# A spectral attention kernel: products of factors and modes in four 64x64 tiles, and sums over modes begun on VectorE

## The chip, the cores and the metric

The kernel runs on one core of a Trainium2 chip. The metric is device time in microseconds; the median of three runs of the kernel before is 557.22 us (555.65 to 564.92). Times inside a run come from one profiled execution, whose span, from the first to the last instruction, is 555.1 us.

## The reference, cut to what matters

Two layers of a Fourier neural operator with attention, over x of shape (2, 56, 128, 128): 2 batches, 56 planes of 128x128. Each layer first normalises groups of pixels and then computes, cut to what matters here:

```
def spectral_conv(x, w, b):                    # M1 = M2 = 16
    xf = jnp.fft.rfft2(x, norm='forward')
    top = jnp.einsum('bihw,iohw->bohw', xf[:, :, :M1, :M2], _c(w[0]))
    bot = jnp.einsum('bihw,iohw->bohw', xf[:, :, -M1:, :M2], _c(w[1]))
    ...
k, q, v = (fno_layer(xn, ...) for K, Q, V)     # back by irfft2, 1x1 skip added; 8 heads
scores = jnp.einsum('baks,bals->bakl', qh, kh) * scale
attn = jax.nn.softmax(scores, axis=-1)
out = jnp.einsum('bakl,bals->baks', attn, vh)
out = fno_layer(out, P)
att = inorm(out + xa, gan, ban)
h = fno_layer(inorm(att, g2, b2), M0, norm=True, act=True)
h = fno_layer(h, M1, norm=True)
y = inorm(h, gmo, bmo) + att                   # the layer adds x to it
```

Only 32x16 complex modes of each plane pass through the weights. So the kernel works on modes: 1024 real numbers per plane, held as 128 partitions by 8 groups of 56 planes.

## The kernel before, in words

For each batch `b` and layer `L` the work is a chain of stages, each written as a Python generator. `_woven` and `_with` mix the generators of two batches; the tile framework then orders the instructions of each engine and places the semaphores, so the order on an engine is not exactly that of the text.

*Modes* (`modes_chain`, L456). Statistics, normalisation, then the transform over the two axes (`to_modes`, L381). The modes of a batch end in `xf` (128 x 448 = 8 groups `t` of 56 planes, and 8 columns of zeros), copied by ScalarE at L498. The two halves of 64 partitions, `e` = 0 and 1, hold different modes.

*Gram* (`gram`, L506 to L514) multiplies every image row with itself, 128 matmuls at L511.

*Scores* (`scores`, L566). For each pair of groups, `t` and `t + 1`, 32 matmuls at L597 multiply 64x64 factors `WU` with the 64x56 modes, for 8 heads, two groups `k` and two halves `e`. The row half of the array is the half of the modes, the column half is the half of PSUM that is written. Before, both are `e`, so of the four 64x64 quadrants of the array only two are in use, in alternation:

```
e = k ^ r
T.matmul(
    p[64 * e : 64 * e + 64, k, K * a : K * a + K], lhsT=WUv[64 * e : 64 * e + 64, t + k, a, :],
    rhs=xv[64 * e : 64 * e + 64, t + k, :], start=True, stop=True,
    tile_position=(64 * e, 64 * e), skip_group_check=True,
)
```

ScalarE copies the 128x896 result out of PSUM (L602) into one of two buffers `UX`; `scored` (L583) multiplies the buffer of two steps earlier by the modes, at L578, and adds up all eight groups in one PSUM bank. A last product (also L578, with `gc`) closes the sum, and L637 on VectorE, the start of the softmax, waits for it. `p` comes from `pair()`, three PSUM buffers of two banks shared by nearly all stages; `bank()` has two of one bank.

*Values, softmax, mix, heads* follow (L611 to L697), with L620 using all four quadrants for 64x256 products, and L680 and L690 for the mixing.

*Norms* (`norms_chain`, L699). The variances of the outputs are sums over the modes, each mode counted twice but those that are their own mirror (`count`, 1 or 2 per partition and group). `sums` (L439) takes 8 matmuls of one column, one per group, with the 56 planes as the stationary side. It is called for `u` (L713) and for the squares `sqy` (L715); L717 on VectorE reads the two columns, L721 takes roots on ScalarE, L431 builds a diagonal, and L436 spreads it over the partitions. The norms of batch 0 run together with the scores of batch 1; the norms of batch 1 run together with `gelu` of batch 0.

*First and second layer of the perceptron* (`gelu`, L771: synthesis L751, mixing L766, GELU L819, statistics L821 on VectorE, turning back L801, transform L789; `h_chain`, L830). In `h_chain`, `sums` is called for s2 and s1 (L852 and L853), after L843 (modes), `multiply` (L419, copied at L424), the squares (L847) and L848; L855 reads the result.

*End* (`end`, L886). L916 on VectorE and L918 on GpSimd make the outputs; `moved` issues their loads and stores on SP's queue (L896). For layer 0 `turned` (L354) brings them into the next layer's form. `prepare` (L235), with L270 to L302, makes the factors of layer 1's weights on GpSimd while layer 0 runs.

SP's queue issues DMAs in order: the image loads, two rows of `gvr` per batch and layer (L554, one per half), then the loads and stores of L896. `P[b]` is one big buffer per batch; its columns are reused: the planes (0 to 7168), `SG` and `MI` of the scores (7168 to 7840), the outputs of the perceptron (all 8192).

Of the kernel before, what the change touches and what calls it, by code (L numbers as in the profile page):

```python
# [39 lines left out]
ALU = mybir.AluOpType  # L40
AX = mybir.AxisListType
# [7 lines left out]
_PARTS = {}  # L49
for _name, _n in (  # L50
    ("ident", N), ("fw", 32), ("fh", N), ("gw", N), ("group", N), ("dup", N), ("ext", N), ("fold", 64),
    ("raw", 56), ("count", 8), ("syn", 1), ("same", 32), ("m8", 8), ("m16", 16), ("n2", 1), ("fx", N), ("gh", 2 * N),
):
    _PARTS[_name] = (sum(n for _, n in _PARTS.values()), _n)
N_CONST = sum(n for _, n in _PARTS.values())
# [2 lines left out]
def _constants():  # L58
    pos = np.arange(N)
    th = 2 * np.pi * np.outer(pos, np.arange(16)) / N  # L60
    fw = np.concatenate([np.cos(th), -np.sin(th)], 1) / N

    def over_h(h):
        ph = 2 * np.pi * np.outer(h, _KY) / N
        cy, sy = np.cos(ph), np.sin(ph)
        return np.concatenate([cy, -sy, sy, cy], 1) / N, np.stack([np.r_[cy.T, -sy.T], np.r_[sy.T, cy.T]], 1)

    at = 4 * (pos % 32) + pos // 32
    fh = over_h(at)[0]
    g, s, e, c = at // 16, at // 8 % 2, at // 2 % 4, at % 2  # L70
    by_layer = []
    for hx, hz in (
        (16 * g + 8 * c + 4 * s + e, pos.reshape(4, 4, 2, 4).transpose(1, 0, 3, 2)),
        (16 * g + 4 * c + 8 * s + e, pos.reshape(4, 2, 4, 4).transpose(2, 0, 3, 1)),
    ):
        z = over_h(hz.reshape(-1))[1]
        by_layer += [over_h(hx)[0], np.concatenate([z, z], 0).reshape(N, 2 * N)]
    twice = np.where(np.arange(16) == 0, 1.0, 2.0)
    both = np.stack([np.cos(th) * twice, -np.sin(th) * twice]).reshape(2, N, 2, 8)
    gw = np.tile(both.transpose(2, 0, 3, 1).reshape(32, N), (4, 1))  # L80
    p = np.arange(N)
    group = (p[:, None] // 4 == p // 4) / 4.0
    k = np.arange(K)
    dup, ext, fold = np.zeros((N, N)), np.zeros((N, N)), np.zeros((N, 64))
    for r in range(2):
        dup[k, 64 * r + k] = 1
        ext[k, 64 * r + k] = 1
        ext[k, 64 * r + K] = -1
        fold[64 * r + k, k] = 1

    c, kx = p // 16 % 2, p % 16
    row = 8 * (p // 32)[:, None] + np.arange(8)
    edge = kx[:, None] == 0
    own = np.where(edge, 0.5, np.ones((N, 8)))
    mirror = np.where(edge & (row != 16), 0.5, np.zeros((N, 8)))
    count = np.where(edge & (row != 16), 1.0, np.full((N, 8), 2.0))
    dc = np.where(edge & (row == 0), 0.0, np.ones((N, 8)))
    re, im = (c == 0)[:, None] * 1.0, (c == 1)[:, None] * 1.0
    raw = np.stack(
        [own, mirror, -mirror, count * dc * N * re, count * dc * N * im, dc * re, dc * im], 1  # L100
    ).reshape(N, 56)

    ky2, e2 = p % 32, p // 64
    edge2 = (8 * e2[:, None] + np.arange(8)) == 0
    parts = {
        "ident": np.eye(N), "fw": fw, "fh": fh, "gw": gw, "group": group, "dup": dup, "ext": ext,
        "fold": fold, "raw": raw,
        "count": np.where(edge2 & (ky2 != 16)[:, None], 1.0, 2.0),
        "syn": np.where(edge2 & (ky2 == 16)[:, None], 2.0, 1.0)[:, :1],
        "same": (ky2[:, None] == np.arange(32)) * 1.0,  # L110
        "m8": (p[:, None] % 8 == np.arange(8)) * 1.0,
        "m16": (p[:, None] // 8 == np.arange(16)) * 1.0,
        "n2": np.full((N, 1), 1.0 / N**2),
    }
    whole = np.concatenate([parts[n] for n in _PARTS if n in parts] + by_layer, 1)
    return {"all": np.ascontiguousarray(whole, np.float32)}
# [50 lines left out]
def fno_layers(ctx: ExitStack, tc: tile.TileContext, x, out, weights, small, const):  # L167
# [19 lines left out]
    def little(name, shape):  # L187
        return sm.tile(shape, F32, name=name)

    def grid(flat, n=8):  # L190
        return flat.rearrange("p (t k) -> p t k", t=n)
# [244 lines left out]
        T.matmul(p[:, : n * K], lhsT=ones[:K, :], rhs=dg, start=True, stop=True)  # L436
        return p[:, : n * K].rearrange("p (n k) -> p n k", n=n)

    def sums(p, col, of, start, stop):  # L439
        for t in range(8):  # L440
            T.matmul(
                p[:K, col : col + 1], lhsT=of[:, K * t : K * t + K], rhs=C["count"][:, t : t + 1],
                start=start and t == 0, stop=stop and t == 7, skip_group_check=True,
            )

    def padded(name, of, row):
# [9 lines left out]
    def modes_chain(L, b, stats, st):  # L456
        mv, gs, gv, sh = (little(f"{n}{b}", [N, k]) for n, k in (("mv", 2), ("gs", 2), ("gv", 1), ("sh", 1)))
        V.bn_aggr(mv, stats.rearrange("p n s -> p (n s)"))
        V.scalar_tensor_tensor(mv[:, 1:2], mv[:, 0:1], mv[:, 0:1], mv[:, 1:2], ALU.mult, ALU.add)
        yield 1.5  # L460
        p = bank()
        T.matmul(p[:, :2], lhsT=C["group"], rhs=mv, start=True, stop=True)
        V.tensor_copy(gs, p[:, :2])
        V.tensor_tensor(gv, gs[:, 0:1], gs[:, 0:1], ALU.mult)
        V.tensor_tensor(gv, gs[:, 1:2], gv, ALU.subtract)
        S.activation(gv, gv, AF.Sqrt, bias=eps)
        V.reciprocal(gv, gv)
        V.scalar_tensor_tensor(sh, gs[:, 0:1], -1.0, gv, ALU.mult, ALU.mult)
        mid = half[b][:, :1792]
        midv = grid(mid, 32)  # L470
        turned_rows = plane[b].rearrange("p (h q) k -> p q h k", q=4)
        wide = P[b][:, 7168 : 7168 + N]
        for j in range(4):
            i = 14 * j
            v = plane[b][:, :, i : i + 14]
            if j % 2:
                S.activation(v, v, AF.Identity, bias=sh, scale=gv)
            else:
                V.tensor_scalar(v, v, gv, sh, ALU.mult, ALU.add)
            yield 3.0 if j == 0 else 0.8  # L480
            p = bank()
            for q in range(4):
                T.matmul(  # L483
                    p[32 * q : 32 * q + 32, :448].rearrange("p (h i) -> p h i", h=32), lhsT=C["fw"],
                    rhs=turned_rows[:, q, :, i : i + 14], start=True, stop=True, tile_position=(0, 32 * q),
                    skip_group_check=True,
                )
            V.transpose(
                midv[:, :, i : i + 14].rearrange("p m i -> p i m"), p[:, :448].rearrange("p (h i) -> p i h", h=32),
            )  # L490
        G.tensor_copy(wide, gv.to_broadcast([N, N]))
        for c in range(2):
            G.tensor_scalar(wide[:, 64 * c + K : 64 * c + K + 1], sh, -1.0, None, ALU.mult)
        yield 2.2
        xf = sp.tile([N, 456], F32, name=f"xf{b}")
        G.memset(xf[:, 448:], 0.0)
        p = to_modes(mid, C["fx"])
        S.copy(xf[:, :448], p)  # L498

        p = bank()  # L500
        T.matmul(p[:, :N], lhsT=wide, rhs=ident, start=True, stop=True)
        gvr = little(f"gvr{b}", [N, N])
        S.copy(gvr, p[:, :N])
        st.update(xf=xf, gvr=gvr)

    def gram(b, st):  # L506

# [58 lines left out]
    def scores(L, b, st):  # L566
# [16 lines left out]
        def scored(t):  # L583
            u = R["UX"][t // 2 % 2]
            for k in range(2):
                score(
                    xf[:, K * (t + k) : K * (t + k) + 64], grid(u[:, 448 * k : 448 * k + 448]), start=(t + k == 0),
                    stop=False,
                )

        for t in range(0, 8, 2):
            p = pair()
            for r in range(2):
                for a in range(HEADS):
                    for k in range(2):
                        e = k ^ r
                        T.matmul(  # L597
                            p[64 * e : 64 * e + 64, k, K * a : K * a + K], lhsT=WUv[64 * e : 64 * e + 64, t + k, a, :],
                            rhs=xv[64 * e : 64 * e + 64, t + k, :], start=True, stop=True,
                            tile_position=(64 * e, 64 * e), skip_group_check=True,  # L600
                        )
            S.copy(R["UX"][t // 2 % 2].rearrange("p (k m) -> p k m", k=2), p[:, :, :448])  # L602
            yield 2.0
# [95 lines left out]
    def norms_chain(L, b, st):  # L699
# [10 lines left out]
        yield 0.8  # L710
        p = bank()
        T.matmul(p[:K, 0:1], lhsT=st["gb"], rhs=C["n2"][:K], start=True, stop=False, skip_group_check=True)
        sums(p, 0, u, False, False)  # L713
        yield 0.4
        sums(p, 1, sqy, False, True)  # L715
        k3, tm = (little(f"{n}{b}", [K, k]) for n, k in (("k3", 3), ("tm", 1)))
        V.tensor_scalar(k3[:, 0:1], p[:K, 0:1], EPS, None, ALU.add)  # L717
        V.tensor_scalar(k3[:, 1:2], p[:K, 0:1], d["gan2"][:K], EPS * EPS, ALU.mult, ALU.add)
# [111 lines left out]
    def h_chain(L, b, st):  # L830
# [18 lines left out]
        yield 1.6  # L849
        p = bank()  # L850
        T.matmul(p[:64, 2:4], lhsT=C["fold"], rhs=mv, start=True, stop=True, skip_group_check=True)
        sums(p, 1, s2, False, False)  # L852
        sums(p, 0, s1, False, True)  # L853
        c4, f1, r3 = little(f"c4{b}", [K, 4]), little(f"f1{b}", [K, 4]), little(f"r3{b}", [K, 2])
        V.tensor_copy(c4, p[:K, :4])  # L855
        g_, f_, u_, w_ = (f1[:, k : k + 1] for k in range(4))
# [168 lines left out]
```

## Time and profile before

| what | value |
|---|---|
| median of three runs | 557.22 us (555.65, 557.22, 564.92) |
| span of the profiled execution | 555.1 us |
| TensorE busy (matmul, weight load) | 457.0 us (82%), 316.3 us (57%) |
| VectorE, ScalarE, GpSimd busy | 337.0, 190.2, 184.3 us |
| mean granted clock of TensorE | 0.901 |
| L597, matmul records and busy time | 1024, 35.9 us |
| L441, matmul records and busy time | 256 (two rows of 128), 7.9 + 7.2 us |
| L578, matmul records and busy time | 144 (128 + 16), 17.5 + 2.4 us |
| HBM traffic | 24.69 MB read, 14.68 MB written |

A row of instruction groups reads: line, engine, operation, output <- inputs, shape and count, then busy time in us and mean ns of one, then how long the engine was idle before them and who ended it. A matmul in fp32 shows as two records, each with a weight load (PEld) and a matmul (PE). The chain of waits is the work that ended last, followed back from the end; its lines are the start in us, the length in us and the work.

### The profile page before, as it was taken

The page shows a single profiled execution, that of the slowest core. Times are in us where ns is not written, and L with a number is a line of the kernel's source. Part 1 is how long each engine was busy: PE and PEld are TensorE (multiplying, and loading weights), DVE is VectorE, ACT ScalarE, POOL GpSimd, SP SyncE. Part 2 cuts the span into 40 slices and gives each one's busy share as a digit, 9 for nine tenths or more (in the row PEclk, how much of TensorE's full clock was granted, in tenths as well). Part 3 has the DMA queues.
Part 4 walks back from the last instruction along what each step waited for, and adds up shares of the span by engine and source line. Part 5 has one row for each costly group of instructions (what it writes and reads, how often), then busy time and mean ns, then how long its engine had stood idle before and what let it go on. Part 6 is the DMA issues. An engine that isn't in the chain of part 4 may idle for free.

```text
span 555.1 us, 14768 instructions
## 1 busy us (share of the span) xinstructions
PE 457.0 (82%) x6630; PEld 316.3 (57%) x6630; DVE 337.0 (61%) x577; ACT 190.2 (34%) x238; POOL 184.3 (33%) x194
## 2 busy tenths in 40 slices
PE   2447889799999999798688859989999999979390
PEld 1423858669685555455563447768967556535250
DVE  0576478932717665869459995841253865677751
ACT  2344132063437556233103314124454656602000
POOL 2460424920271000065456871630000000035566
PEclk9999689899998999988667959989999999988586
DMA  8993000050000000056144541030000000017687
GB/s 202 213 197 58 4 2 2 5 145 4 2 3 1 1 2 1 1 166 198 53 132 133 168 127 14 2 105 4 2 2 2 1 1 2 2 33 225 191 230 285
DMA packets 16303, 40.58 MB, mean 73 GB/s; under 512 B 2528, under 2 KB 3296, under 8 KB 16224
## 3 DMA queue, kind: packets, MB, share of 16 engines
q1 hardware_dynamic: 15520, 38.25, 25.5%
q10 hardware_dynamic: 720, 1.39, 1.0%
q8 instruction: 52, 0.85, 0.6%
q14 instruction: 11, 0.09, 0.1%
HBM read 24.69 MB, written 14.68 MB: 71 GB/s over the span
## 4 chain that ended last, share of the span: by engine, by line
PE 43%; DVE 26%; DMA 8%; ACT 7%; POOL 7%; issue 5%; SPq 2%; POOLq 0%; ACTq 0%; DVEq 0%
PE pair L766 5%; DVE X L550 4%; PE pair L801 4%; PE pair L751 4%; PE pair L597 4%; DVE stats L373 4%; PE bank L511 3%; PE bank L578 3%; DMA C<-const_all 3%; DMA X<-store 3%; POOL P L918 3%; PE bank L690 3%; PE bank L789 2%; PE bank L483 2%; DMA xr<-store 2%
## 5 line engine op out<-in xcount | busy, mean ns | idle before, releaser
L821 DVE BATCH_NORM_STATS2 stats<-P 128x6 f32<-128x512 f32 x64 | 40.5, 681 | 19.3 <-ACT P L819 19.2
L916 DVE SCALAR_TENSOR_TENSOR P<-P,hs,pair 128x1024 f32<-128x1024 f32 x32 | 40.0, 1269 | 18.7 <-PE pair L766 18.7
L918 POOL TENSOR_TENSOR X<-P,xr 128x1024 f32<-128x1024 f32 x16 | 39.9, 2500 | 30.5 <-DVE P L916 16.5
L550 DVE TENSOR_TENSOR X<-X,gvr 120x1024 f32<-120x1024 f32 x32 | 49.3, 1568 | 0.0
L373 DVE BATCH_NORM_STATS2 stats<-P 128x6 f32<-128x448 f32 x64 | 35.7, 610 | 20.1 <-ACT P L368 10.1
L819 ACT ACTIVATE P<-pair 128x1024 f32<-128x1024 f32 x32 | 32.6, 1026 | 32.0 <-PE pair L766 31.3
L395 POOL MEMSET WT<- 128x256 f32 x4 | 1.3, 313 | 121.0 <-PE bank L789 88.3
L766 PE MATMUL pair<-X,Be 57*64 57x512 f32 x256 | 41.1, 742 | 0.0
L511 PEld LDWEIGHTS bank<-P 128*64 128x64 f32 (+1 forms) x1024 | 37.1, 158 | 2.9 <-issue 2.6
L511 PE MATMUL bank<-P 128*64 128x56 f32 (+1 forms) x1024 | 38.7, 244 | 0.0
L801 PEld LDWEIGHTS pair<-C,P 120*128 120x128 f32 x256 | 26.8, 143 | 20.9 <-issue 12.3
L766 PE MATMUL pair<-X,Bs 57*64 57x512 f32 x256 | 37.5, 627 | 0.0
L751 PE MATMUL pair<-C,WT 32*128 32x128 f32 x512 | 26.7, 319 | 11.3 <-DVE P L916 5.5
L597 PE MATMUL pair<-xf,WU 64*64 64x56 f32 x1024 | 35.9, 220 | 0.0
L597 PEld LDWEIGHTS pair<-xf,WU 64*64 64x64 f32 x1024 | 32.8, 134 | 5.0 <-issue 3.9
L751 PEld LDWEIGHTS pair<-C,WT 32*128 32x128 f32 x512 | 21.6, 214 | 23.6 <-issue 9.1
L801 PE MATMUL pair<-C,P 120*128 120x120 f32 x256 | 34.3, 277 | 0.4 <-ACT P L819 0.2
L341 POOL TENSOR_TENSOR WT<-tc,C 128x1024 f32<-128x1024 f32 x8 | 26.5, 3341 | 20.0 <-ACT tc L335 11.9
L802 ACT COPY WT<-pair 128x896 f32<-128x896 f32 x32 | 28.8, 906 | 12.5 <-PE pair L801 12.3
L363 PE MATMUL pair<-C,X 56*128 56x56 f32 x256 | 17.5, 292 | 18.6 <-DMA X<-x 12.8
L371 ACT COPY P<-pair 128x896 f32<-128x896 f32 x16 | 14.4, 902 | 46.7 <-PE pair L365 46.7
L365 PE MATMUL pair<-C,X 120*128 120x120 f32 x128 | 20.3, 313 | 10.2 <-POOL X L918 9.2
(249 smaller groups left out, 868.8 us busy)
## 6 DMA issues: line engine op xcount, KB each, us to landing
X<-x SPq DMA_DIRECT2D x16, 448.0 KB
xr<-x SPq DMA_DIRECT2D x32, 224.0 KB
store<-X SPq DMA_DIRECT2D x32, 224.0 KB
out<-P SPq DMA_DIRECT2D x32, 224.0 KB
xr<-store SPq DMA_DIRECT2D x16, 224.0 KB
X<-store SPq DMA_DIRECT2D x16, 224.0 KB
C<-const_all ACTq DMA_DIRECT2D x1, 621.0 KB
stage<-weights ACTq DMA_DIRECT2D x1, 544.0 KB
```

The costliest lines, as they stand in the source:

```text
L373: V.bn_stats(stats[:, 2 * g + s, :], dst[:, 448 * s : 448 * s + 448])
L511: T.matmul(p[u : u + m, :K], lhsT=P[b][:, K * i : K * i + m], rhs=plane[b][:, i, :], start=(i < 2), stop=(i == N - 1), tile_position=(0, u ...
L550: V.tensor_tensor(v, v, _bc(st["gvr"][:120], 1, 8), ALU.mult)
L597: T.matmul(p[64 * e : 64 * e + 64, k, K * a : K * a + K], lhsT=WUv[64 * e : 64 * e + 64, t + k, a, :], rhs=xv[64 * e : 64 * e + 64, t + k, ...
L751: T.matmul(both[j // 2][:, j % 2, N * e : N * e + N], lhsT=Z[32 * j : 32 * j + 32, o : o + N], rhs=C["gw"][32 * j : 32 * j + 32, :], start ...
L766: T.matmul(p[64 * c : 64 * c + 64, r, :], lhsT=Bs[q, :], rhs=X2[q, b, s : s + 4, :].rearrange("p e w -> p (e w)"), start=False, stop=True, ...
L801: T.transpose(p[:, r, N * e : N * e + 120], h3[:120, o : o + N], ident[:120, :120])
L802: S.copy(hT[v].rearrange("p r e c k -> p (r e) c k"), p.rearrange("p r (e c k) -> p (r e) c k", e=4, c=2)[:, :, :, :K],)
L819: S.activation(h3, both[v].rearrange("p r m -> p (r m)"), AF.Gelu)
L821: V.bn_stats(stats[:, 4 * A + 2 * v + r, :], h3[:, 512 * r : 512 * r + 512])
L916: V.scalar_tensor_tensor(h3, h3, st["hs"], both[v].rearrange("p r m -> p (r m)"), ALU.mult, ALU.add)
L918: G.tensor_tensor(dst, h3, back(n), ALU.add)
```

## The change

Three things.

1. *Four quadrants.* At L597 the loop runs over heads, then `k`, then `e`, and the PSUM half is `o = e ^ k`: an even group is written to the half it came from, an odd one to the other. Four matmuls in a row use the four quadrants.
2. *A copy of the modes with swapped halves.* As the odd groups of the product lie in the other half, L578 needs the modes of odd groups there too: `xs`, columns 7840 to 8072 of `P[b]`, is filled by two DMAs on SP's queue right after `xf`, and its last 8 columns are zeroed on GpSimd.
3. *Sums.* `sums` adds the eight groups on VectorE first, into a 128x56 tile, and then takes two matmuls of one column: the added groups with 2.0, and the first group with -1.0 where a mode is its own mirror. The constant `count` shrinks from 8 columns to 2.

The diff, cut to its core:

```
-        "count": np.where(edge2 & (ky2 != 16)[:, None], 1.0, 2.0),
+        "count": np.concatenate([np.full((N, 1), 2.0), -1.0 * (edge2 & (ky2 != 16)[:, None])[:, :1]], 1),
...
-    def sums(p, col, of, start, stop):
-        for t in range(8):
+    def sums(p, col, of, start, stop, name):
+        r = little(name, [N, K])
+        V.tensor_reduce(r, of.rearrange("p (t k) -> p k t", t=8), AX.X, ALU.add)
+        for j, part in enumerate((of[:, :K], r)):
             T.matmul(
-                p[:K, col : col + 1], lhsT=of[:, K * t : K * t + K], rhs=C["count"][:, t : t + 1],
-                start=start and t == 0, stop=stop and t == 7, skip_group_check=True,
+                p[:K, col : col + 1], lhsT=part, rhs=C["count"][:, 1 - j : 2 - j], start=start and j == 0,
+                stop=stop and j == 1, skip_group_check=True,
             )
...
         S.copy(xf[:, :448], p)
+        xs = P[b][:, 7840:8072]
+        G.memset(xs[:, 224:], 0.0)
+        for e in range(2):
+            q, o = slice(64 * e, 64 * e + 64), slice(64 - 64 * e, 128 - 64 * e)
+            nc.sync.dma_start(
+                out=xs[o, :224].rearrange("p (u k) -> p u k", k=K),
+                in_=xf[q, :448].rearrange("p (u v k) -> p u v k", v=2, k=K)[:, :, 1, :],
+            )
...
                 score(
-                    xf[:, K * (t + k) : K * (t + k) + 64], grid(u[:, 448 * k : 448 * k + 448]), start=(t + k == 0),
-                    stop=False,
+                    (xf[:, K * t : K * t + 64], st["xs"][:, K * t // 2 : K * t // 2 + 64])[k], grid(u[:, 448 * k : 448 * k + 448]),
+                    start=(t + k == 0), stop=False,
                 )
...
-            for r in range(2):
-                for a in range(HEADS):
-                    for k in range(2):
-                        e = k ^ r
+            for a in range(HEADS):
+                for k in range(2):
+                    for e in range(2):
+                        o = e ^ k
                         T.matmul(
-                            p[64 * e : 64 * e + 64, k, K * a : K * a + K], lhsT=WUv[64 * e : 64 * e + 64, t + k, a, :],
+                            p[64 * o : 64 * o + 64, k, K * a : K * a + K], lhsT=WUv[64 * e : 64 * e + 64, t + k, a, :],
                             rhs=xv[64 * e : 64 * e + 64, t + k, :], start=True, stop=True,
-                            tile_position=(64 * e, 64 * e), skip_group_check=True,
+                            tile_position=(64 * e, 64 * o), skip_group_check=True,
                         )
```

The four calls of `sums` (L713, L715, L852, L853) get a tile name as well. In the order that the framework gives the built kernel, the memset of L395 for batch 1 in layer 0 stands ahead of L270 and L271 on GpSimd, and the second sum of batch 1 at L715 has its reduce behind four statistics of L821 on VectorE. Lines after the edits move by 2 to 10; L597 becomes L607, L578 L588, L441 L443 and the reduce is L441.

More of the change, by code (lines that the diff above doesn't have):

```diff
@@ L51 @@
     ("ident", N), ("fw", 32), ("fh", N), ("gw", N), ("group", N), ("dup", N), ("ext", N), ("fold", 64),
-    ("raw", 56), ("count", 8), ("syn", 1), ("same", 32), ("m8", 8), ("m16", 16), ("n2", 1), ("fx", N), ("gh", 2 * N),
+    ("raw", 56), ("count", 2), ("syn", 1), ("same", 32), ("m8", 8), ("m16", 16), ("n2", 1), ("fx", N), ("gh", 2 * N),
 ):
@@ L503, in modes_chain @@
         S.copy(gvr, p[:, :N])
-        st.update(xf=xf, gvr=gvr)
+        st.update(xf=xf, xs=xs, gvr=gvr)
     def gram(b, st):
@@ L712, in norms_chain @@
         T.matmul(p[:K, 0:1], lhsT=st["gb"], rhs=C["n2"][:K], start=True, stop=False, skip_group_check=True)
-        sums(p, 0, u, False, False)
+        sums(p, 0, u, False, False, f"ru{b}")
         yield 0.4
-        sums(p, 1, sqy, False, True)
+        sums(p, 1, sqy, False, True, f"rq{b}")
         k3, tm = (little(f"{n}{b}", [K, k]) for n, k in (("k3", 3), ("tm", 1)))
@@ L851, in h_chain @@
         T.matmul(p[:64, 2:4], lhsT=C["fold"], rhs=mv, start=True, stop=True, skip_group_check=True)
-        sums(p, 1, s2, False, False)
-        sums(p, 0, s1, False, True)
+        sums(p, 1, s2, False, False, f"ru{b}")
+        sums(p, 0, s1, False, True, f"rq{b}")
         c4, f1, r3 = little(f"c4{b}", [K, 4]), little(f"f1{b}", [K, 4]), little(f"r3{b}", [K, 2])
```

## Prediction

> **What bounds the kernel now.** I read the page first: its chain of waits is 43% TensorE and 26% VectorE, so neither engine is the bound everywhere and each stage has to be looked at alone. The two rows of the product that the change rearranges:
>
> ```profile
> L597 PE MATMUL pair<-xf,WU 64*64 64x56 f32 x1024 | 35.9, 220 | 0.0
> L597 PEld LDWEIGHTS pair<-xf,WU 64*64 64x64 f32 x1024 | 32.8, 134 | 5.0 <-issue 3.9
> ```
>
> 1024 records stand for 512 matmuls: an fp32 matmul shows as two records (the program issues 4 steps x 32 matmuls x 2 batches x 2 layers). They keep TensorE busy for 36 us, but the page's chain gives L597 only 4%, some 20 us. Only those 20 us can be saved directly. So next, the chain in order of time, at the scores of batch 1, layer 0:
>
> ```profile
> 132.19 1.14 PE pair L419 x32
> 133.33 1.87 PE pair L597 x64
> 135.19 0.86 PE bank L441 x15
> 136.06 0.86 PE bank L578 x8
> 136.92 0.78 PE bank L441 x16
> 137.70 2.00 PE pair L597 x64
> 139.71 0.91 PE bank L578 x8
> 140.61 2.00 PE pair L597 x64
> 142.62 0.48 PE bank L436 x2
> 143.10 2.00 PE bank L578 x18
> ```
>
> For 13 us TensorE alone carries the path, and the softmax (L637, 145.33) waits for its last matmul. The same ten rows stand at 392.24 to 403.15 for layer 1. Both things that the change touches, L597 and the sums (L441), lie here. The sums of the second perceptron layer are on the path too:
>
> ```profile
> 207.03 1.10 PE pair L751 x32
> ...
> 208.66 1.02 PE pair L766 x8
> 209.67 0.21 PE bank L851 x2
> 209.88 1.67 PE bank L441 x32
> ```
>
> **What sets the pace of L597.** From chain rows: L441 loads 56 columns into one tile and takes 1.67/32 = 52 ns a record, 0.93 ns a column. L597 takes 1.87/64 = 29.2 ns a record with two tiles side by side, so 58 ns for each tile, 0.91 ns per column of its 64-column load: weight loads set its pace. Do four quadrants load and stream side by side? L766 is such a case: 1.02/8 = 128 ns a record of 512 columns, 0.25 ns a column; L578 with two tiles of 224 columns takes 0.86/8 = 108 ns, 0.48 ns. Four tiles are nearly twice as fast as two. L751 (four row tiles, loads of 128 columns) takes 1.10/32 = 34 ns, so loads overlap as well. And where the last L597 of one burst meets L620, which uses all four quadrants, the timeline has both in the same 60 ns:
>
> ```profile
> 109.88 0.43 PE L620 MATMUL pair<-WT,xf 64*64 64x256 f32 x2
> 109.93 0.23 PE L597 MATMUL pair<-xf,WU 64*64 64x56 f32 x2
> ```
>
> What no row shows is a long run faster than 29 ns a record.
>
> **What the Trainium skill says.** "TensorEngine Tiling (Array Packing)", Key Properties: tiles work independently, and different ones load and multiply at once; the rows above agree. "TensorE: Matmul & The Clock Gate", The mechanism: weight loads overlap running matmuls only if their row groups differ. The trace differs: L511 (128x64, both tiles on all rows) does 36 records in 1.19 us, 33 ns, like L597. Same page, "Wait — 56ns, not 53.3ns?": matmul starts don't come closer than about 25 ns; no stretch here tells. "SBUF — State Buffer", Who interferes with whom: tensor_reduce never contends with GpSimd, but two-input VectorE instructions do; the latter is seen (L861, one column, took 2.18 us under L918).
>
> **The change, part by part.**
>
> *Quadrants.* If a round of four takes the 58 ns of a round of two, 64 records take 0.93 us, not 1.87 to 2.00. Bounds: 0.93 (full overlap), 1.60 (25 ns a record, an estimate from the page), 1.87 (none). I take 0.95.
>
> *Sums.* 16 calls; each loses 16 records (0.83 us) and keeps 4 (0.21), and gains one reduce of 448 elements with a stride of 56. Nearest row: L639, a contiguous reduce of 224 in 377 ns; L702, 448 elements in 624. So 0.65 at pace 1, and about 1.1 if the stride costs double, which no row shows; I take 0.8.
>
> *Copy of the modes.* Two DMAs per batch and layer on SP's queue, and two little memsets on POOL. Nearest row: L554, also SBUF to SBUF, issue 0.56 us each; landing I put at 2 to 4 us (the page "DMA: Bandwidth & Descriptors", Anatomy of one DMA, has a fixed 2.0). Cover, layer 0: the modes are copied at 54.3 and 84.4, and L578 first needs them at 111.4 and 136. Layer 1: SP reaches the first pair after the loads of 322.3, L578 reads at 367; the second waits for the modes (351.5), L578 reads it at 396. Queued behind them: four stores that wait for POOL until 327 anyway, and a row of X2 that L766 needs after 422. Cost 0; without cover, about 3 us each.
>
> *POOL.* By the built order, the memset at L395 of batch 1 goes ahead of L270 and L271 in the preparation of layer 1's weights (layer 0 only). It waits for L664 (155.39), so two multiplies of 1.35 us move behind it and the preparation ends 2.7 us later. Waiting for it: the copy bm (L709), due at L733 (177), some 7 us later. Cost 0, and 2.7 us if that cover were gone.
>
> **The sum,** against the profiled span of 555.1 us.
>
> Scores of batch 1 (twice): I replay the order. L419 ends 133.33; L597 to 134.3; first sum, its reduce done at 134.25, to 134.5; L578 to 135.35; second sum: the square ends at 134.57, reduce to 135.4, matmuls to 135.6; L597 to 136.6; L578 137.4; L597 138.4 (copy L602, 0.91 us, free in time); L436, whose diagonal is ready 2.5 us after the second sum, at 138.4, to 138.9; 20 records of L578 and its closing product to 141.1. Before 145.3, so 4.2; I take 4.1, for hand-overs that I have not counted.
>
> Scores of batch 0: layer 0: 84 records of L597 end 1.3 us earlier, but L331 needs L324, which VectorE ends at 87.12: 1.1. At 108.6 and after, 32 records, partly under the row scaling (L550): 0.3. Layer 1: at 340.7 L483 waits for VectorE's L479 (343.12) anyway: 0.1; at 371.1, 34 records: 0.7.
>
> Norms of batch 1 (twice), a loss: the second reduce stands behind four L821, whose end is where TensorE can first get its sum:
>
> ```profile
> 166.50 2.64 DVE L821 BATCH_NORM_STATS2 stats<-P 128x6 f32<-128x512 f32 x4 [1.79 <-ACT P L819]
> 168.33 1.06 PE L441 MATMUL bank<-C,P 128*56 128x1 f32 x16 [0.23 <-ACT P L705]
> ```
>
> 169.14 + 0.8 + 0.2 = 170.15 against 169.4: -0.8; L766, L801 and the factors of the norm queue behind it.
>
> Second perceptron layer: batch 0 (twice): s2 ends at 208.28, two reduces to 209.9, sums to 210.3 against 211.55; ACT's table load (210.78 to 212.06) and L802 eat part: +0.8. Batch 1: the reduces delay L916 by 1.6 us and the sums end about when they did: 0. In layer 1 this lies under the DMA loop of the end.
>
> Total: layer 0: 1.4 + 4.1 - 0.8 + 0.8 = 5.5; layer 1: 0.8 + 4.1 - 0.8 + 0.8 = 4.9; together 10.4 us: a span of 544.7. The median of the runs shown (557.22) is 2.1 above the span; I forecast 557.2 - 10.4 = 546.8 us. Everything after the scores waits for them, down to the DMA loop at 495, which starts from its predecessor; so nothing is given back there.
>
> **Rivals.**
> 1. *An issue limit* near 25 ns a record. For: no row is below 29. Against: the meeting of L597 and L620. L597 then saves 14% and not half: its share of the gain (1.4 + 0.8 + 2 x 2.6 = 7.4 us) falls to 2.1, that of the sums (3.0) stays: about 552.
> 2. *No overlap*, tiles of one row half wait for each other as the page on TensorE says: L597 as before, 557.2 - 3.0 = 554. Against it: L511.
> 3. *Slower: the four tiles run one after another*, because odd steps now put two row halves into one PSUM bank and each tile's two passes block the next. 58 ns a record, 3.7 us for 64. On the path are 20/1.87 = 10.7 bursts: +20 - 3.0, about 574. It is slower by over 2% once a burst takes 3.2 us. Against: L651 has two row halves in one bank, and 16 records took 0.68 us.
> 4. *A dear reduce* of 1.1 us and more: 2 to 3 us less gain, about 549.
>
> **How the numbers follow.** Main case 0.66, issue limit 0.14, no overlap 0.08, serial tiles 0.09, dear reduce 0.03. The main case's own range is 542 to 550: reduces of 0.65 or 1.1, bursts of 0.93 to 1.05, and 2 us more if VectorE's chain at 250 to 259, which waits for POOL, slips in ahead of it. The range, 542 to 555, takes in cases 1, 2 and 4 and leaves out serial tiles. 2% is 11.1 us, about what a measurement of this kernel tells from no change; the limit, 546.1, cuts the main case: faster by over 2%: 0.66 x 0.54 = 0.36. Slower: 0.09 and a little for a wait that I don't see: 0.11. Within: 0.53.
>
> **What would show it.** L597 with about 18 us busy for 1024 records and bursts of 64 in under 1.1 us; L637 of batch 1 some 4 us sooner after L419; the reduce at 0.65 to 1.1 us; TensorE idle just before the second sum of batch 1; no wait of L578 for a DMA. I am wrong if bursts stay at 1.87 us, if L578 waits for the copied modes, or if the later stages don't keep the 4 us.

## The result, and the profile after

The median goes from 557.33 to 550.33 us; the ratio is 0.986, with a 95% interval of 0.982 to 0.990, so 5 to 10 us are gained by this count. A second series of the same kernel gave 0.985 (0.981 to 0.988). The profiled execution has a span of 548.9 us, 6.2 less than before. The ratios leave out executions more than 1.5% above the fastest of their kernel, which takes away 15 of the 22 of the second series (544.6 to 560.1 us) but only 1 of the 27 of the kernel before beside them. Over all of these the means are 557.1 and 554.0 us, a gain of 3.0 us (+-2.0), and the median of the 22 is 555.3. So the ratio flatters a kernel whose executions spread widely. Below I give ratios with intervals, the means of all executions where they say something else, and above all stage times.

The groups of the product, from the list of instruction groups by shape, matmuls and then weight loads (before: 35.9 and 32.8 us):

```profile
L607 PE MATMUL pair<-xf,WU 64*64 64x56 f32 x1024 | 22.4, 228 | 0.0
L607 PEld LDWEIGHTS pair<-xf,WU 64*64 64x64 f32 x1024 | 18.9, 140 | 5.6 <-issue 4.6
```

The chain of waits at the scores of batch 1, layer 0 (start, length, work):

```profile
131.27 0.64 DVE P L717
...
131.93 1.01 DVE ru L441
...
132.99 0.21 PE bank L443
133.20 0.86 PE bank L588 x8
134.06 0.30 PE bank L443 x4
134.36 1.08 PE pair L607 x64
135.45 0.91 PE bank L588 x8
136.35 1.08 PE pair L607 x64
137.44 0.48 PE bank L436 x2
137.92 2.00 PE bank L588 x18
```

Set this beside the ten lines of before. A burst of 64 records takes 1.08 us for 1.87 to 2.00, and only two bursts are left on the chain, since the first now runs while VectorE is still at its squares and the first reduce. In these bursts the four matmul records of a round start 6 to 7 ns apart and the rounds follow each other every 58 ns, as the rounds of two did before: 16 x 58 = 0.93 us, and 0.15 us to the end of the last one. The new price is also in view: the reduce stands on the chain with 1.01 us.

The second perceptron layer of batch 0 goes as forecast: two reduces and the last six matmul records for the 1.67 us of 32 records.

```profile
204.07 0.97 DVE rq L441
205.04 0.90 DVE ru L441
...
205.98 0.48 PE bank L443 x6
```

At the norms of batch 1 the second reduce stands behind four L831 (before: L821), as forecast. VectorE's timeline:

```profile
161.30 2.64 DVE L831 BATCH_NORM_STATS2 stats<-P 128x6 f32<-128x512 f32 x4 [0.64 <-ACT P L829]
163.85 0.96 DVE L441 TENSOR_REDUCE rq<-P 128x56 f32<-128x448 f32 x1
165.16 0.15 DVE L727 TENSOR_SCALAR k<-bank 56x1 f32<-56x1 f32 x1 [0.35 <-PE bank L443]
...
165.60 0.94 DVE L730 SCALAR_TENSOR_TENSOR k<-k,tm 56x1 f32<-56x1 f32 x1
```

The last line was not in the forecast: one column took 0.94 us, where before it took 0.15. More on it below.

And L588 (before: L578) waits for no DMA; the view of that line lists all that it waited for:

```profile
its engine sat idle before it (us, times) until:
  issue: 2.5, 8
  ACT P L612: 0.4, 1
```

How much the changed kernel gains on before in each step, by starts of the same VectorE instructions in both traces (us, + is gained; line numbers of before). Row one counts from the start of the span in layer 0 and from L521 of batch 0 in layer 1, at 312.50 us in the trace of before. The last two columns are from the first experiment; the execution traced for the quadrants alone took 557.9 us.

| step | forecast, layers 0 and 1 | changed, 0 and 1 | quadrants alone | sums alone |
|---|---|---|---|---|
| scores of batch 0, up to L637 | +1.4, +0.8 | +1.56, +1.41 | -0.17, -0.41 | -0.31, +0.03 |
| scores of batch 1, L702 to L637 | +4.1 each | +3.63, +3.44 | +2.77, +2.77 | +1.24, +1.24 |
| norms of batch 1, L637 to L717 | -0.8 each | -0.92, -1.00 | +0.09, +0.01 | -0.92, -1.08 |
| second layer, batch 0, L848 to L855 | +0.8 each | +0.88, +0.88 | 0, 0 | +0.88, +0.88 |
| second layer, batch 1, L848 to L855 | 0 each | -1.96, +0.30 | -0.54, 0 | -2.33, +0.40 |

Row four is +0.88 in every trace that has both its strided reduces. Row two is 3.62 or 3.63 in layer 0 of all eight traces with the four quadrants in batch 1 and the strided reduces, the reordered product row_pairs among them; in layer 1 four of them have 3.61 to 3.63 too, and the four in which batch 1 takes all four sums with reduces have 2.96 to 3.46. There the second burst ends late, by 0.18 us in the changed kernel and 0.67 at most, and the profile shows no releaser. Why is open. Row three repeats to 0.1 us where no half-clock window (a stretch in which TensorE was granted half its clock) falls into it. Rows one and five don't repeat, and the experiments ask why.

### The profile page after: what moved, and what is told of

Its sections match the earlier page's. It is cut to its first block, busy times and chain, and to the rows that moved or that the text cites. A ratio compares the mean times of both kernels' runs of the same rounds, so it can differ in the third digit from the quotient of the medians.

```text
span 548.9 us, 14430 instructions
## 1 busy us (share of the span) xinstructions
PE 440.6 (80%) x6438; PEld 296.4 (54%) x6438; DVE 350.6 (64%) x593; ACT 189.6 (35%) x238; POOL 180.4 (33%) x198
## 4 chain that ended last, share of the span: by engine, by line
PE 46%; DVE 30%; ACT 8%; issue 7%; POOL 4%; DMA 3%; POOLq 1%; ACTq 0%; DVEq 0%
PE pair L776 8%; PE pair L761 5%; PE pair L811 5%; DVE X L560 4%; DVE stats L373 4%; PE bank L521 4%; PE bank L700 3%; DMA C<-const_all 3%; DVE P L926 3%; PE bank L485 3%; PE bank L588 3%; PE bank L799 2%; DVE WT L406 2%; PE bank L386 2%; POOL P L928 2%
## 5 line engine op out<-in xcount | busy, mean ns | idle before, releaser
L831 DVE BATCH_NORM_STATS2 stats<-P 128x6 f32<-128x512 f32 x64 | 40.5, 680 | 17.3 <-ACT P L829 17.1
L521 PE MATMUL bank<-P 128*64 128x56 f32 (+1 forms) x1024 | 40.5, 250 | 0.0
L521 PEld LDWEIGHTS bank<-P 128*64 128x64 f32 (+1 forms) x1024 | 38.9, 164 | 2.2 <-issue 1.9
L395 POOL MEMSET WT<- 128x256 f32 x4 | 1.3, 314 | 114.5 <-PE bank L799 88.8
L761 PE MATMUL pair<-C,WT 32*128 32x128 f32 x512 | 29.3, 336 | 11.1 <-DVE P L926 5.3
L761 PEld LDWEIGHTS pair<-C,WT 32*128 32x128 f32 x512 | 24.0, 229 | 23.4 <-issue 9.3
L363 PEld LDWEIGHTS pair<-C,X 56*128 56x128 f32 x256 | 14.9, 197 | 24.0 <-DMA X<-x 10.0
L365 PEld LDWEIGHTS pair<-C,X 120*128 120x128 f32 x128 | 16.1, 163 | 21.2 <-POOL X L928 11.6
```

What stands on the lines that cost most here:

```text
L363: T.transpose(p[:, c, o : o + K], X2[q, b, i, :], ident[q, q], tile_position=(64 * c, 0))
L365: T.transpose(p[:, s, N * e : N * e + 120], X2[:120, b, i, :], ident[:120, :120])
L521: T.matmul(p[u : u + m, :K], lhsT=P[b][:, K * i : K * i + m], rhs=plane[b][:, i, :], start=(i < 2), stop=(i == N - 1), tile_position=(0, u ...
L761: T.matmul(both[j // 2][:, j % 2, N * e : N * e + N], lhsT=Z[32 * j : 32 * j + 32, o : o + N], rhs=C["gw"][32 * j : 32 * j + 32, :], start ...
L831: V.bn_stats(stats[:, 4 * A + 2 * v + r, :], h3[:, 512 * r : 512 * r + 512])
```

## The experiments

*1. The two parts apart.* One kernel keeps the quadrants and the swapped copy, the other only the new sums:

```
quadrants_alone:  sums() and "count" as in the kernel before
sums_alone:       L597, L578 and xf as in the kernel before
```

> Keeps the four quadrants and the swapped copy of the modes; the sums are the sixteen matmuls of before. Theory (from the two traces): a round of four tiles takes 58 ns like a round of two before, and the sums paid for themselves only in batch 0. Then L597 has about 18 us busy, the scores of batch 1 end 2.6 us sooner after L419 than before (three bursts of 1.08 us for 1.87 to 2.00), nothing is lost at the norms of batch 1 or in the second perceptron layer of batch 1, and the time is about 549 us, no worse than the changed kernel's 550.3. Rival (the sums carry a good part of the gain, as in the blind sum, where they bring 3.0 of 10.4 us): slower than the changed kernel by about 3 us, 553.

> Keeps the product in two quadrants and only begins the sums on VectorE. Theory: per layer about +1.0 us at the norms of batch 0 and +0.9 at the second perceptron layer of batch 0, but -1.0 at the norms of batch 1 and -2.7 (layer 0) and about -1.2 (layer 1) in the second perceptron layer of batch 1 and what follows: together -2 us, 557 to 560 us. Rival (the blind sum): +3.0 us, 554.

Measured: the quadrants alone give 0.986 (0.981 to 0.990), the same as both together; the sums alone 1.002 (0.999 to 1.004), nothing. Over all its 22 executions the kernel with the sums alone is even 2.5 us (+-1.6) slower than before. In rows two to four each kernel shows its own gains and losses and not the other's. The theory held as far as such times can tell: the gain is the product's, and what the sums add lies within the intervals. By rows two to four the sums bring 1.24 + 0.88 - 0.9 = 1.2 us per layer, 2.4 in all; row five takes most of it back in this trace (-2.33 and +0.40). Beside the four quadrants they add less at the scores (3.6 - 2.8 = 0.8 us), because there the reduce is what TensorE waits for.

*2. Sums on VectorE only where they help.*

```
-        sums(p, 0, u, False, False, f"ru{b}")
+        sums8(p, 0, u, False, False) if b else sums(p, 0, u, False, False, f"ru{b}")
```

`sums8` is the old loop of eight matmuls. In the first kernel this is done at all four calls, in the second only at s2 and s1:

> The changed kernel, but in batch 1 all four sums are the matmuls of before; VectorE adds only for batch 0. Theory: the reduces of batch 1 stand in VectorE's order ahead of work that GpSimd and the transforms wait for; without them the losses of 1.0 us twice, 2.7 and about 1.2 us go, and the time is 544 to 546 us. In the trace the copy L855 of batch 1 in layer 0 stays about 5 us ahead of the kernel before, where the changed kernel had 3.2. Rival: the loss in the second perceptron layer is an accident of phase (a two-input VectorE multiply meets the GpSimd addition and takes 2.2 us for 0.63) and stays: 548 us.

> The changed kernel, but the two sums of the second perceptron layer of batch 1 are the matmuls of before; the norms keep theirs. Theory: the 2.7 us of layer 0 and some 1 us of the end come back, 546 to 547 us; the norms of batch 1 still lose 1.0 us per layer. Rival (accident of phase): 549 to 550 us, with the multiply L848 of batch 1 at 2.2 us.

Measured: 0.987 (0.982 to 0.992) and 0.991 (0.987 to 0.995). The loss at the norms is gone in the first (+0.08 and +0.02 us to L717) and there in the second (-1.02 and -1.01). In both, L855 of batch 1 keeps its lead. But neither time shows the 4 to 6 us that my theory had given back. A part of what I had charged to the reduces was one multiply, L848 of batch 1, and GpSimd's addition L918. Timelines of VectorE and GpSimd, first the changed kernel, then the kernel with sums for batch 0 (its L866 is the same multiply):

```profile
242.04 2.35 POOL L928 TENSOR_TENSOR X<-P,xr 128x1024 f32<-128x1024 f32 x1 [3.00 <-DVE stats L373]
242.66 2.21 DVE L858 TENSOR_TENSOR WU<-WU,xf 128x448 f32<-128x448 f32 x1 [0.62 <-ACT WU L424]
```

```profile
243.23 0.63 DVE L866 TENSOR_TENSOR WU<-WU,xf 128x448 f32<-128x448 f32 x1 [0.62 <-ACT WU L425]
```

The multiply lies inside the addition and takes 2.21 us for 0.63: 1.6 of the 1.96 us of the table. "SBUF — State Buffer", Who interferes with whom, in the Trainium skill, has this: two-input VectorE instructions and GpSimd's reads share a port, a reduce does not; the strided reduces did stay within 0.95 to 1.00 us in all ten traces that have them, also where GpSimd was at work (the reduce at 163.85 us above ran beside the preparation); two-input instructions did not.

*3. Steady or by chance?* The changed kernel and the one of experiment 2 once more, with no edit.

> The changed kernel as it is, once more. Two theories of the 4 us by which it falls short of the blind sum. A (the reduces of batch 1 are a steady loss): the stages repeat, with about 1.0 us lost at the norms of batch 1 in each layer and 2.0 to 2.7 in the second perceptron layer of batch 1 in layer 0, and the ratio to before stays near 0.986. B (phase): the multiply L848 of batch 1 meets the GpSimd addition in some executions and not in others (0.63 against about 2.2 us), and the half-clock windows of TensorE fall on other stages in each execution; then only the 1.0 us at the norms repeats, and among the executions the time follows the mean granted clock by some 3 us per 0.01.

> The kernel that lets VectorE add for batch 0 only, once more, beside the changed kernel on one chip. Theory A (the reduces of batch 1 are a steady loss of 2 x 1.0 us at the norms and 2 to 3 in the second perceptron layer): 4 to 5 us faster than the changed kernel, about 546. Theory B (only the norms are steady): about 2 us faster, 548 to 549, too little to be told apart by the time, but seen in the stages.

Measured: 0.985 (0.981 to 0.988) and 0.987 (0.981 to 0.993): no difference. The multiply took 1.19 us in the one and 0.63 in the other, the norms again lost 0.92 and 1.00 us in the one and, in layer 1, nothing in the other. In layer 0 of the latter a half-clock window of 6.8 us falls into the norms, so that stage says nothing. So theory B: the loss at the norms is steady, the collision is not. Over the 22 executions the time follows the mean clock more steeply than expected, by 5 us per 0.01 for the 3. A second trace of the kernel before settles that the collision isn't the change's:

> The kernel before, for a second trace of it. Theory of the clock: in the scores of batch 0 of layer 0 at most one window of 3.4 us at half clock, as in the first trace. Rival (phase alone): windows of 7 to 10 us there too, as in several traces of the changed kernel.

```profile
247.89 2.35 POOL L918 TENSOR_TENSOR X<-P,xr 128x1024 f32<-128x1024 f32 x1 [4.08 <-DMA xr<-x]
247.94 2.78 DVE L848 TENSOR_TENSOR WU<-WU,xf 128x448 f32<-128x448 f32 x1 [0.62 <-ACT WU L424]
```

Here the kernel before has it too, with 2.78 us. In its first trace the multiply started first, and then it was GpSimd's addition that grew, to 2.71 us:

```profile
247.72 0.63 DVE L848 TENSOR_TENSOR WU<-WU,xf 128x448 f32<-128x448 f32 x1 [0.62 <-ACT WU L424]
247.85 2.71 POOL L918 TENSOR_TENSOR X<-P,xr 128x1024 f32<-128x1024 f32 x1 [4.23 <-DMA xr<-x]
```

GpSimd had waited for a DMA, and whether it starts just before or just after VectorE differs from execution to execution. In layer 1 the same multiply took 2.48 us in both traces of before and 1.20 in the changed kernel's: there the collision favours the change. The second trace of before had one window of 6.8 us at half clock in batch 0's scores, between the two expectations.

*4. What sets the pace of the product.* The same 32 matmuls in the same quadrants, in two other orders:

```
row_half_by_row_half:  for e in range(2): for a in range(HEADS): for k in range(2):
row_pairs:             for a in range(HEADS): for e in range(2): for k in range(2):
```

> The changed kernel with the loop over e outermost at the product: the same 32 matmuls in the same four quadrants, but the sixteen of row half 0 first and then those of row half 1, so that two column tiles of one row half alternate. Theory (tiles load and stream side by side whatever row half they are in, and a round of n tiles takes 58 ns): rounds of two again, a burst of 64 records takes 1.87 us as before, L597's counterpart is about 36 us busy, and the time is 556 to 559. Rival (weight loads run beside matmuls only of another row half, as the page on TensorE says): 2.5 to 3.7 us a burst, 565 or more.

> The changed kernel with the loops over k and e exchanged: a round of four quadrants in the order (0,0), (0,1), (1,1), (1,0), so that neighbours share a row half or a column half. Theory (four tiles are independent whatever their order): bursts of 64 records take 1.08 us as in the changed kernel, and its counterpart of L597 is 20 to 22 us busy. Rival (neighbours that share a half wait for each other): 1.5 to 1.9 us a burst.

Measured, from the chains of waits at the scores of batch 1, layer 0 (the second burst of row_pairs, at 143.09, took 1.08 us too):

```profile
141.05 1.82 PE pair L607 x63
142.87 0.91 PE bank L588 x8
143.78 1.83 PE pair L607 x63
```

```profile
141.10 1.08 PE pair L607 x64
142.19 0.91 PE bank L588 x8
```

Two column tiles of one row half alternate at 29 ns a record, just as two tiles on the diagonal did before; a round of four takes 58 ns in either order. So in these three orders what counts is how many different tiles stand in a row in the program: neighbours in one row half don't wait for each other, and both rivals fell by the bursts. The product is busy for 34.4 and 22.7 us, near the 36 and the 20 to 22 expected. The total times, 565.4 and 561.6 us, are of one execution each, at a clock of 0.874 and 0.872, and I read nothing from them, though the first is what the rival had forecast.

*5. What the stride costs the reduce.*

```
-        V.tensor_reduce(r, of.rearrange("p (t k) -> p k t", t=8), AX.X, ALU.add)
+        V.tensor_reduce(r, of.rearrange("p (k t) -> p k t", t=8), AX.X, ALU.add)
```

> The changed kernel with the reduce read contiguously: it adds eight neighbouring columns in place of the eight groups, so the variances are of other sums; all else stands. Theory (the reduce pays for its stride of 224 bytes): 0.97 us fall to about 0.65 to 0.75, the pace of the contiguous reduces of the softmax. Rival (pace and fixed cost are the same for any stride, and the many short results cost): 0.95 to 1.0 us as in the changed kernel.

Lines of the reduce, min/median/max in ns, first of the changed kernel, then of this one:

```profile
L441 DVE TENSOR_REDUCE ru<-P x4: 985/993/1004, 131.9 to 416.0; 128x56 f32<-128x448 f32 x4
```

```profile
L441 DVE TENSOR_REDUCE ru<-P x4: 619/620/621, 136.5 to 416.5; 128x56 f32<-128x448 f32 x4
```

The theory held: the stride costs 0.37 us, 60%. Pace 1 (0.62 us for 448 elements) was the right floor, and the change pays above it. This kernel adds up the wrong elements, so its reduce alone is read.

*6. Is the clock the rest?* The mean granted clock over the executions compared is 0.904 for before (77) and 0.897 for the changed kernel (10); over all executions with a recorded clock it is 0.903 (79) and 0.891 (26). The traces show only full and half clock, in windows of 3.4 us or several. My theory was that the shorter product leaves TensorE idle in batch 0's scores, where VectorE sets the pace. In the first kernel batch 0 takes its matmuls in an order in which only two quadrants alternate; the second adds to it the sums of experiment 2:

```
+            heads = [(a, k) for a in range(HEADS) for k in range(2)]
+            for a, k in heads if b else sorted(heads, key=lambda h: h[1]):
```

> The changed kernel, but in batch 0 the product runs first through the even group of the pair and then through the odd one, so that only two of the four quadrants alternate at a time; batch 1 keeps the four, and the number of instructions is the same. The runs of the changed kernel so far have a lower mean granted clock than those of before (0.890 against 0.905), and their time follows it. Theory (a shorter product leaves TensorE idle longer in the scores of batch 0, where VectorE sets the pace, and the next 3 to 10 us run at half clock): batch 0's bursts take 1.87 us again under the cover of VectorE, the mean clock returns to 0.90 or more and the mean of all runs falls from 554 to about 550 to 552 us. Rival (the clock falls for another reason: the sums on VectorE, or the phase of the clock's windows alone): mean clock 0.89, and the mean time no better than 554.

> Both cuts at once: the product uses four quadrants at a time only in batch 1 and two in batch 0, and VectorE begins the sums only in batch 0. Theory (the steady gains are 3.6 us per layer in the scores of batch 1 and 0.9 in the second perceptron layer of batch 0, 9.0 in all; the losses are 1.0 per layer at the norms of batch 1 and a lower clock where a short product leaves TensorE idle in batch 0): mean clock 0.895 to 0.905, all runs within some 8 us of each other, median 548 to 550 us, and both steady gains in the trace at 3.6 and 0.9 us with no loss at the norms. Rival (the clock of the changed kernel is lower by phase or for a reason that lies elsewhere): a mean clock of 0.89 and a median of 552 or more.

Measured: ratios of 0.989 (0.985 to 0.993) and 0.992 (0.989 to 0.995), mean clock 0.897 and 0.898. Here nothing was left out, neither of the 6 and 7 executions nor of before's 10 and 12 beside them, and the answer depends on what is counted:

| kernel | ratio | gain over all executions, us | mean clock over all | fastest to slowest, us |
|---|---|---|---|---|
| changed, second series | 0.985 | 3.0 (+-2.0) | 0.890 | 544.6 to 560.1 |
| two tiles in batch 0 | 0.989 | 6.0 (+-2.1) | 0.897 | 550.2 to 556.5 |
| and sums in batch 0 only | 0.992 | 4.6 (+-1.6) | 0.898 | 550.3 to 556.5 |

By the ratios the second, which I had thought the best of all, is slower than the changed kernel (0.981 to 0.988); by all executions neither is. The clock rose by 0.007 to 0.008, less than the theory asked of the first (0.90) and more than the rival allowed (0.89). For the second, the clock and the spread came out as the theory had them and the median, 553.1 us, as the rival had it, although its trace has both steady gains (+3.62 at the scores of batch 1, +0.88 twice, nothing lost at L717). It ran on another chip, where before had a clock of 0.899 itself. Nor do the pairs agree: over all executions the first is ahead of its counterpart with four quadrants in batch 0 too (6.0 for 3.0 us), the second behind its own (4.6 for 6.8 and 5.1), all within the intervals. So the theory is neither shown nor refuted, and whether the four quadrants in batch 0 gain anything stays open.

## Why the prediction was right

*The mechanism.* Rounds of four at the pace of rounds of two: right to the nanosecond (58). The bursts are 1.08 us and not 0.95, since I left out the end of the last round, 0.15 us. L607 has 22.4 us busy and not 18. Half-clock windows are about 1.2 us of that: the two traces with four quadrants throughout and no record of L607's counterpart in such a window (sums_batch0_again, no_reduce_h1) have 21.2. The rest I put down to bursts that run in pieces between other matmuls, which was not measured apart. Rivals 1, 2 and 3 fall with it: starts 6 to 7 ns apart, 29 ns a record in one row half, no burst near 3.7 us.

*Scores of batch 1: 3.6 and 3.4 us for 4.1.* The two mis-sized terms are the burst (1.08 for 0.95) and the reduce (0.97 to 1.01 for 0.8); in layer 1 the stall of 0.18 us comes on top. Rival 4 named this price, a dear reduce, at 1.1 us: in size it lies between my value and the rival's.

*Norms of batch 1: -0.92 and -1.00 for -0.8*, by the same 0.2 us of the reduce; the step, with TensorE idle before the second sum, is as forecast.

*Second layer, batch 0: +0.88 for +0.8.* Right.

*Second layer, batch 1: 0.* The step said that the sums end about when they did. Without the collision they do in layer 0, within 0.4 us (from the multiply's end to L855: 2.87 us after, 2.49 before). The collision took 1.6 us in the changed kernel's trace; it belongs to both kernels, so it explains that trace and not the ratio.

*POOL: cost 0, and here the step failed.* I asked who waits for the preparation's data, the copy bm, and found 7 us of cover. I did not ask whom GpSimd disturbs while it runs. Before, its last preparation instruction ran at 168.88 and L720 on VectorE at 169.86. After, the memset of L395 came at 150.18 and not at 155.39, so the preparation does not end 2.7 us later as I had it, but 0.5 us sooner (its last instruction starts at 168.34). The norms come 4.3 us sooner, so L730 at 165.60 falls into it:

```profile
169.86 0.15 DVE L720 SCALAR_TENSOR_TENSOR k<-k,tm 56x1 f32<-56x1 f32 x1
```

```profile
165.92 0.32 POOL L287 TENSOR_TENSOR stage<-stage,C 128x64 f32<-128x64 f32 x1
```

L730 takes 0.94 us for 0.15, and the lead falls from 4.26 us at L720 to 3.47 at L722. Of the eleven traces with the swapped copy and its order on GpSimd, ten show 0.82 to 1.93 us here and one 0.15; both traces of before and that of the sums alone show 0.15. The loss stays: from L717 of batch 1 to the next L848 of batch 0 it is 37.03 to 37.05 us in the three traces with neither this collision nor a half-clock window, and 38.18 in the one with a collision of 1.29 us and no window. (Before's first trace lost as much there to a window, 38.23 us, so the comparison of the two first traces hides it.) That the preparation is the cause is argued from the overlap alone: no run moved it away, and in the trace of the sums alone one small instruction of it (128x16) overlaps a start of L720 that still took 0.15 us.

*The copy of the modes: 0.* Right: no wait of L588 for a DMA. How long the two copies took to land, no view here shows.

*Sum.* Forecast 10.4 us; the ratios say 7.7 (5 to 10) and 8.4 (6.5 to 10), all executions of the second series 3.0 (+-2.0). About 1.1 us are the burst and the reduce at the scores (0.5 and 0.7, the second with the stall), 0.3 the norms, 0.8 L730. Most of the rest goes with the clock, for which the sum has no term. An estimate of it: fitted with one common slope over the executions that the ratios use, the time falls by 2.2 us (+-0.5) per 0.01 of mean clock, and at equal clock the change would be worth 10.0 us (+-1.1). Over all executions the slope is 3.1 us (+-0.4) and the worth 7.9 us (+-1.1), which agrees with 10.4 less the 2.2 just named; I trust it more, since leaving out long executions flattens the slope. By it the clock's 0.013 between the two kernels take back about 4 us. Why the changed kernel gets the lower clock is not shown: experiment 6 doesn't settle it.

*Luck.* The range of 542 to 555 us took in the forecasts of three rivals (552, 554, 549), so the time alone doesn't speak for the mechanism; the bursts do. And the first median, 550.3, lies in the range, while that of the 22 executions of the second series, 555.3, lies just outside. That the time came out right is in part the luck of four executions.

## What to carry to other kernels

If a run of small matmuls is paced by its weight loads, count how many different tiles of the array stand next to each other in the program; going from two to four took a run from 1.87 to 1.08 us, and nothing about their rows or PSUM halves mattered. Moving a sum to an idle engine pays only where that engine is not itself waited for: 16 reduces of 1 us in place of 96 of 128 matmuls brought this kernel nothing that the ratio could show (1.002), and over all executions it was 2.5 us slower. When a stage gets earlier, look at what it now runs beside: a one-column VectorE instruction beside GpSimd's took 0.8 to 1.9 us here, as much as a whole reduce. And when executions of one program spread by 3%, count all of them as well as the fastest: the change is worth 8 us by one count and 3 by the other.

## What the runs showed of the hardware

The times follow TensorE's half-clock windows (over the 22 executions of the second series, time and mean clock correlate with -0.86): their grid stands differently to the program in each execution (the first long one began at 56.5 us in the trace of before, at 60.8 in that of the changed kernel, at 58.5 with sums for batch 0 only). Of two traces of that last kernel, one had windows of 10.2, 3.4, 3.4 and 6.8 us up to L637 of batch 0 and reached it at 120.25 us; the other had 6.8 and 10.2 us and reached it at 113.96. Equal stages of equal kernels thus differ by nearly as much as the whole change is worth; only stages free of such windows, compared from marker to marker, told the parts apart.
